# Cross-attention's softmax division moved from the attention result to the output weight's products, and its key sums taken with a column of ones

## The chip, the cores and the metric

One core of a Trainium2 chip runs the whole program. The metric is device time in microseconds of that core, as the median of several executions. The unprofiled executions of the kernel before lie between 1841.42 and 1842.9 us.

## The reference, cut to what matters

A decoder of two layers works on `x` of 4 batches, 256 tokens, 256 features. The first five sublayers and the last one are: rotary self-attention, cross-attention to `ctx` without weights, a ternary feed-forward, a gated recurrence, then the cross-attention that the change is in, then a mixture of 8 experts with the best 2 taken. The cross-attention of the second layer, with 16 query heads of 128 features that share 4 key and value heads, is:

```python
q = (draft_hidden @ Wq.T).reshape(bsz, draft_len, H, HD)         # H = 16, HD = 128, 256 queries
q = _rms_norm(q, q_norm_w).transpose(0, 2, 1, 3)
kv_in = jnp.concatenate([context_hidden, draft_hidden], axis=1)  # 1601 + 256 = 1857 keys
k = (kv_in @ Wk.T).reshape(bsz, total_len, KVH, HD)              # KVH = 4
v = (kv_in @ Wv.T).reshape(bsz, total_len, KVH, HD).transpose(0, 2, 1, 3)
k = _rms_norm(k, k_norm_w).transpose(0, 2, 1, 3)
q = _rope(q, draft_position_ids)
k = _rope(k, full_position_ids)
k = jnp.repeat(k, N_REP, axis=1)                                 # N_REP = 4
v = jnp.repeat(v, N_REP, axis=1)
scores = jnp.einsum('bhqd,bhkd->bhqk', q, k) * SCALE
probs = jax.nn.softmax(scores, axis=-1)
attn = jnp.einsum('bhqk,bhkd->bhqd', probs, v)
attn = attn.transpose(0, 2, 1, 3).reshape(bsz, draft_len, H * HD)
return attn @ Wo.T                                               # added to x by the caller
```

The mixture of experts follows it per batch and needs the finished `x` of that batch.

## The kernel before, in words

Everything is float32. Up to about 500 us four generators, one for each batch, run the first four sublayers interleaved. After that comes the cross-attention, which takes the largest part of the time.

The cross-attention loops over 16 "heads" `(b, g)`: batch `b`, key-value head `g`. Each has two `Pair` objects, `h = 0` and `h = 2`, and a pair holds two query heads with 256 queries each, so 512 query columns. There are 32 pairs. The 1857 keys are in 15 chunks of up to 128, taken two at a time in `NPAIR = 8` steps.

- `Pair.score(c)` multiplies a chunk of keys by the 512 queries into a PSUM bank `bsc` (L1181). ScalarE copies it to `s` with the key's norm as the scale (L1182), and VectorE keeps a running maximum `acc` over chunks (L1186). Keys stand on partitions, queries on the free axis.
- `Pair.maximum()` transposes `acc` (`tm`, L1193), takes the maximum of each query (`mq`, L1195) and spreads it again over partitions into the bank `bc` (L1199).
- `Pair.exponential(c)` subtracts `bc` (VectorE, L1203), takes the exponential (ScalarE, L1206) and adds it to `sum` (GpSimd, L1212), a 128 by 512 tile that has one partial sum for each partition of keys.
- `Pair.weigh(c)` multiplies values by `s` into the bank `po` (L1221): 128 value features on partitions, 512 queries on the free axis.
- `Pair.finish()` is what the change is in. It copies `po` to `aT` (ScalarE, L1228). It transposes the four 128-column blocks of `sum` into a bank `ts` (L1232), so that queries stand on partitions, reduces over the free axis (VectorE, L1234) and takes the reciprocal `rs` (L1235). It spreads `rs` over partitions by four transposes into a bank `rb` (L1239) and multiplies `aT` by it (L1240). In pair `h = 2` of a head, all four query heads' `aT` are multiplied by the output weight `wo` into one bank `bpw`, accumulating over the four heads (L1247), and one VectorE add puts the bank into `x` (L1252).

A float32 product is two TensorE instructions in the trace; a transpose is one.

Between these, a head's successor is prepared: `prep_q` (queries, `pq` L1078, rotary, then `ACT L1047` scales by a norm that GpSimd works out at L1043, then `tpq` L1090 and the copy L1091) and `prep_kv` (keys and values, `pk` L1115, rotary, `tpk` L1124, and the copy of the keys `kTb` by ScalarE, L1126). The experts of the batch before run in 23 steps (`mph` L914, `mpe` L925, and an addition to `x` of a product scaled per token, L927).

The order of all this is written out by hand. Work runs in steps `s`; a step has two places, `2s` after the scores and `2s + 1` after the weighing. `put(place, gen, last, bank)` books the next part of a generator at a place; with `bank=True` it takes the first place from there on that no other booking with `bank=True` holds. [...] 32 places make one head, and a head lasts about 82 us in the trace.

[...] one for `bc`, one for `po`, and six that `p1(...)` hands out in turn. So a bank from `p1` can be written only when what was handed out six requests earlier has been read. `ts`, `rb`, `bpw`, `bsc`, `tm`, `pq`, `pk`, `tpk`, `mph` and `mpe` all come from `p1`.

`load_wo` loads the head's output weight; its booking is 15 places ahead of the place of `rb` in the pair `h = 0`.

Of the kernel before, what the change touches and what calls it, by code (L numbers as in the profile page):

```python
# [16 lines left out]
ALU = mybir.AluOpType  # L17
AX = mybir.AxisListType
PSUM = bass.MemoryType.PSUM

P = 128
# [88 lines left out]
def decoder_kernel(ctx: ExitStack, tc: tile.TileContext, at, t, out):  # L110
    nc = tc.nc
    V, A, G, T = nc.vector, nc.scalar, nc.gpsimd, nc.tensor
# [18 lines left out]
    def p1(name):  # L131

        ring[0] += 1
        if psb and ring[0] % 3 == 0:
            return psb[0].tile([P, 512], F32, tag="one", name=name, bufs=2)
        return psa.tile([P, 512], F32, tag="one", name=name, bufs=4)
# [17 lines left out]
    def fa(b, name, dt=F32):  # L154

        return fr.tile([P, 512], dt, tag=f"a{b}", name=name, bufs=NA)
# [9 lines left out]
    def sm(shape, tag, name, bufs=2, dt=F32):  # L166
        return small.tile(shape, dt, tag=tag, name=name, bufs=bufs)
# [3 lines left out]
    xs = [const.tile([P, 2, D], F32, tag=f"x{b}", name=f"x{b}") for b in range(B)]  # L171
# [14 lines left out]
    def cc(name):  # L186
        o, n = at[name]
        return cst[:, o : o + n]

    ident = cc("ident")  # L190
# [768 lines left out]
    def angles(b):  # L959

        d = bt.setdefault(b, {})
        pi = wk.tile([P, NCH], I32, tag="pi", name=f"pi{b}")
        nc.sync.dma_start(out=pi, in_=t["pos"][b])
        if b == 0:
            V.tensor_scalar(knw, knw, math.sqrt(HD1), None, ALU.mult)
        pf = wk.tile([P, NCH], F32, tag="pf", name=f"pf{b}")
        V.tensor_copy(pf, pi)
        sh = [P, NCH, 64]
        ang, sn = (
            fr.tile([P, 960], F32, tag=n, name=f"{n}{b}")[:, 0 : NCH * 64].rearrange(  # L970
                "p (a b) -> p a b", a=NCH
            )
            for n in ("ang", "sn")
        )
        V.tensor_mul(ang, pf[:, :, None].to_broadcast(sh), cc("invf")[:, None, :].to_broadcast(sh))
        yield
        V.tensor_scalar(sn, ang, 1.0 / (2 * math.pi), ROUND, ALU.mult, ALU.add)
        yield
        V.tensor_scalar(sn, sn, ROUND, None, ALU.subtract)
        yield  # L980
        for c in TWO_PI:
            V.scalar_tensor_tensor(ang, sn, -c, ang, ALU.mult, ALU.add)
            yield
        V.tensor_scalar(ang, ang, PI_LO, -PI_LO, ALU.min, ALU.max)
        yield
        A.activation(sn, ang, AF.Sin)
        A.activation(ang, ang, AF.Abs)
        A.activation(ang, ang, AF.Sin, bias=hpi, scale=-1.0)
        d["angles"] = (ang, sn)
        yield  # L990

    def tables(b, only="kq"):

        d = bt[b]
        ang, sn = d["angles"]
        for nm, n, w in (("k", NCH, knw), ("q", 2, qnw)):
            if nm not in only:
                continue
            tb = [P, n, 64]
            ctab = wk.tile([P, n, HD1], F32, tag=f"c{nm}", name=f"ctab{nm}{b}")  # L1000
            stab = wk.tile([P, n, HD1], F32, tag=f"s{nm}", name=f"stab{nm}{b}")
            wlo, whi = w[:, None, 0:64].to_broadcast(tb), w[:, None, 64:128].to_broadcast(tb)
            d[nm] = (ctab, stab)
            V.tensor_mul(ctab[:, :, 0:64], ang[:, 0:n, :], wlo)
            V.tensor_mul(ctab[:, :, 64:128], ang[:, 0:n, :], whi)
            yield

            V.scalar_tensor_tensor(stab[:, :, 64:128], sn[:, 0:n, :], -1.0, whi, ALU.mult, ALU.mult)
            V.tensor_mul(stab[:, :, 0:64], sn[:, 0:n, :], wlo)
            yield  # L1010
# [149 lines left out]
    class Pair:  # L1160
# [62 lines left out]
        def finish(self):  # L1223
            b, g, nm = self.b, self.g, self.nm
            e, su = gt[b, g], self.sum
            aT = fa(1, f"aT{nm}")
            e[self.h] = aT
            A.copy(aT, self.po)  # L1228
            yield
            ts = p1(f"ts{nm}")  # L1230
            for i in range(4):
                T.transpose(ts[:, i * P : (i + 1) * P], su[:, i * P : (i + 1) * P], ident)  # L1232
            rs = sm([P, 4], "rs", f"rs{nm}")
            V.tensor_reduce(rs, ts.rearrange("p (i k) -> p i k", i=4), AX.X, ALU.add)  # L1234
            V.reciprocal(rs, rs)  # L1235
            yield
            rb = p1(f"rb{nm}")
            for i in range(4):
                T.transpose(rb[:, i * P : (i + 1) * P], rs[:, i : i + 1].to_broadcast([P, P]), ident)  # L1239
            V.tensor_mul(aT, aT, rb)  # L1240
            yield
            if self.h == 2:
                pw = p1(f"bpw{b}{g}")
                for j in range(2):
                    for h in range(4):
                        o = (h % 2) * 256 + j * P
                        T.matmul(  # L1247
                            pw[:, j * 256 : j * 256 + 256], lhsT=e[h - h % 2][:, o : o + P], rhs=e["wo"][:, h, :],
                            start=h == 0, stop=h == 3,
                        )  # L1250
                xf = xs[b].rearrange("p j d -> p (j d)")
                V.tensor_add(xf, xf, pw)  # L1252


    heads = [(b, g) for b in range(B) for g in range(NKV)]
# [11 lines left out]
    def put(place, gen, last=False, bank=False):  # L1267
        while bank and place in taken:
            place += 1
        if bank:  # L1270
            taken.add(place)
        places.setdefault(place, []).append((gen, last))
        return place

    def loader(b, g):
        load_wo(b, g)
        yield

    def tokens(b):
        normed_tokens(b)  # L1280
        yield
        bt[b]["xh"] = bt[b]["centred"]()
        yield
        token_features(b)
        yield

    for n, pair in enumerate(pairs):
        e = NPAIR * n + NPAIR - 1
        gen = pair.maximum()
        put(2 * e + 2, gen, bank=True)  # L1290
        put(2 * e + 5, gen, True)
        e += DW
        gen = pair.finish()
        put(2 * e + 1, gen)
        put(2 * e + 4, gen, bank=True)
        put(2 * e + 7, gen, pair.h == 0, bank=True)
        if pair.h:
            put(2 * e + 10, gen, True, bank=True)
    for k, (b, g) in enumerate(heads):
        base = 32 * (k - 1)  # L1300
        if k:
            if g == 0:
                gen = angles(b)
                for i in range(9):
                    put(base - 81 + 6 * i, gen, i == 8)
                gen = tokens(b)
                for i, o in enumerate((-8, -6, -3)):
                    put(base + o, gen, i == 2, i == 2)
                for o, n in ((-5, "q"), (-3, "q"), (7, "k"), (11, "k")):
                    gen = tables(b, n) if o in (-5, 7) else gen  # L1310
                    put(base + o, gen, o in (-3, 11))
            for f, when in ((prep_q, QA), (prep_kv, KA)):
                for i, o in enumerate(when):
                    gen = f(b, g, i)
# [4 lines left out]
        gen = loader(b, g)  # L1319
        put(base + 60, gen, True)  # L1320
    for b in range(B - 1):
        gen = experts(b)
# [145 lines left out]
```

## Time and profile before

| what | value |
|---|---|
| median of the executions | 1842.06 us (1841.42 to 1842.9) |
| profiled execution, its own time | 1839.59 us |
| span in its profile | 1837.7 us |
| what lies around the span | 1.89 us |
| granted TensorE clock, mean | 0.971 |
| TensorE matmul busy | 1727.6 us (94%) |
| VectorE busy | 1288.4 us (70%) |
| ScalarE busy | 1007.2 us (55%) |
| GpSimd busy | 871.8 us (47%) |

A profile is of one execution. Its span is from the first to the last instruction; the time of that execution adds what lies around it. The profiled execution is 2.47 us below the median of the unprofiled ones, so a difference worked out from the profile is subtracted from or added to the median as it stands. The row of an instruction gives its duration from start to end; TensorE overlaps one instruction with the next, so its pace is read from the starts of successive instructions and not from durations. PE is TensorE's matmul, PEld its weight load, DVE is VectorE, ACT ScalarE, POOL GpSimd and SP SyncE, which issues the DMAs.

### The profile page before, as it was taken

How to read it: one execution, taken by the hardware profiler on the slowest of the kernel's cores; microseconds unless marked ns; L12 is line 12 of the kernel's file. 1: busy time of each engine (PE TensorE's matmuls, PEld its weight loads, DVE VectorE, ACT ScalarE, POOL GpSimd, SP SyncE). 2: the span in 40 equal slices, each digit the busy share in tenths (PEclk: the TensorE clock that was granted, in tenths of full speed). 3: DMA queues.
4: the chain of work that ended last, by engine and by line, in shares of the span. 5: the costliest groups of instructions: out<-in, count | busy, mean ns of one | idle time of the engine just before them, and what ended most of it. 6: DMA issues, size and time to landing. Idle time of an engine off the chain costs nothing.

```text
span 1837.7 us, 20229 instructions
## 1 busy us (share of the span) xinstructions
PE 1727.6 (94%) x6576; PEld 1051.1 (57%) x6576; DVE 1288.4 (70%) x2396; ACT 1007.2 (55%) x1896; POOL 871.8 (47%) x716
## 2 busy tenths in 40 slices
PE   4779899989999999999999999999999999999997
PEld 3456786655555554645555555656565655656555
DVE  5785647787777677777767786776768676766754
ACT  1556536464656555675656566565746465555631
POOL 2100232111277566566656465555647574555560
PEclk8789899999999999999999999999999999999998
DMA  4010231100210110102010111201111211111110
GB/s 139 1 39 17 73 119 61 32 24 25 67 55 15 52 34 33 38 30 65 17 62 27 63 35 49 61 29 55 34 62 33 68 38 52 32 35 44 32 38 23
DMA packets 66216, 83.00 MB, mean 45 GB/s; under 512 B 6460, under 2 KB 49600, under 8 KB 66112
## 3 DMA queue, kind: packets, MB, share of 16 engines
q1 hardware_dynamic: 64960, 80.31, 14.1%
q10 hardware_dynamic: 1152, 1.41, 0.2%
q8 instruction: 53, 0.87, 0.2%
q14 instruction: 51, 0.42, 0.1%
HBM read 80.65 MB, written 1.05 MB: 44 GB/s over the span
## 4 chain that ended last, share of the span: by engine, by line
PE 72%; DVE 10%; ACT 8%; POOL 6%; issue 4%; POOLq 0%; DVEq 0%; ACTq 0%
PE bsc L1181 18%; PE bpo L1221 17%; PE pk L1115 11%; POOL sum L1212 3%; PE bpw L1247 3%; PE mph L914 2%; PE xpo L607 2%; ACT s L1206 2%; PE xsc L562 2%; ACT s L1182 2%; PE pq L1078 2%; PE mpe L925 1%; ACT sm L463 1%; PE pp L689 1%; PE tpk L1124 1%
## 5 line engine op out<-in xcount | busy, mean ns | idle before, releaser
L1212 POOL TENSOR_TENSOR sum<-sum,s 128x512 f32<-128x512 f32 (+1 forms) x416 | 541.0, 1301 | 81.9 <-ACT s L1206 55.5
L1181 PE MATMUL bsc<-qTb,kTb 128*128 128x512 f32 (+1 forms) x960 | 457.9, 597 | 3.3 <-ACT kTb L1126 3.3
L1221 PE MATMUL bpo<-s,vb 128*128 128x512 f32 (+1 forms) x960 | 456.0, 593 | 0.0
L1182 ACT ACTIVATE s<-bsc,kn 128x512 f32<-128x512 f32 (+1 forms) x480 | 317.8, 685 | 186.1 <-PE bsc L1181 164.4
L1186 DVE SCALAR_TENSOR_TENSOR acc<-bsc,kn,acc 128x512 f32<-128x512 f32 x448 | 333.6, 745 | 110.0 <-ACT s L1182 100.4
L1203 DVE TENSOR_TENSOR s<-s,bc 128x1024 f32<-128x1024 f32 (+1 forms) x256 | 288.4, 1141 | 14.2 <-PE bc L1199 14.0
L1206 ACT ACTIVATE s<-s 128x1024 f32<-128x1024 f32 (+1 forms) x256 | 256.1, 1009 | 60.7 <-DVE s L1203 59.9
L1181 PEld LDWEIGHTS bsc<-qTb,kTb 128*128 128x128 f32 (+1 forms) x960 | 172.1, 187 | 187.8 <-issue 145.8
L1221 PEld LDWEIGHTS bpo<-s,vb 128*128 128x128 f32 (+1 forms) x960 | 173.4, 191 | 141.3 <-issue 136.6
L1040 POOL TENSOR_TENSOR ropek<-ropek,ropuk 128x512 f32<-128x512 f32 (+1 forms) x64 | 76.9, 1201 | 255.9 <-DVE ropuk L1035 255.9
L1115 PE MATMUL pk<-wkv,cTk 128*128 128x256 f32 x832 | 190.1, 379 | 0.0
L1115 PEld LDWEIGHTS pk<-wkv,cTk 128*128 128x128 f32 x832 | 156.7, 190 | 28.4 <-issue 6.2
L1209 POOL TENSOR_TENSOR sum<-s 128x512 f32<-128x512 f32 x32 | 41.8, 1306 | 186.7 <-ACT s L1206 186.7
L1034 DVE TENSOR_TENSOR ropek<-pk,ctabk 128x256 f32<-128x256 f32 (+1 forms) x128 | 51.8, 404 | 70.6 <-ACT squares L1033 69.9
L1033 ACT ACTIVATE squares<-pk 128x256 f32<-128x256 f32 (+1 forms) x128 | 48.1, 377 | 96.3 <-PE pk L1115 74.7
L1047 ACT ACTIVATE ropeq<-ropeq,rnq 128x128 f32<-128x128 f32 x128 | 41.9, 390 | 107.4 <-POOL rnq L1043 107.4
L1184 DVE TENSOR_SCALAR acc<-bsc,kn 128x512 f32<-128x512 f32 x32 | 24.0, 749 | 83.5 <-ACT s L1182 83.5
L1118 ACT COPY vb<-pk 128x256 f32<-128x256 f32 (+1 forms) x128 | 46.3, 362 | 58.7 <-DVE ropuk L1035 56.0
L463 ACT ACTIVATE sm<-sc,mx 128x128 f32<-128x128 f32 (+1 forms) x128 | 52.2, 435 | 26.5 <-DVE mx L456 19.6
L1043 POOL TENSOR_TENSOR kn<-ssk,nhalf 128x4 f32<-128x4 f32 (+1 forms) x64 | 65.5, 1024 | 0.0
L914 PE MATMUL mph<-yTm,wi 128*128 128x256 f32 x256 | 63.2, 392 | 0.0
L1040 POOL TENSOR_TENSOR ropeq<-ropeq,ropuq 128x512 f32<-128x512 f32 x32 | 41.1, 1284 | 40.5 <-DVE ropuq L1035 40.5
(491 smaller groups left out, 2482.8 us busy)
## 6 DMA issues: line engine op xcount, KB each, us to landing
cTk<-in_ctxT SPq DMA_DIRECT2D x32, 512.0 KB, 3.6
wq<-in_wq SPq DMA_DIRECT2D x16, 512.0 KB, 4.9
wo<-in_wo SPq DMA_DIRECT2D x16, 512.0 KB, 4.0
wi<-in_wi SPq DMA_DIRECT2D x32, 256.0 KB, 2.9
xcT<-in_ctxT SPq DMA_DIRECT2D x12, 512.0 KB, 3.7
xct<-in_ctx SPq DMA_DIRECT2D x12, 512.0 KB, 3.7
cTk<-in_ctxT SPq DMA_DIRECT2D x16, 384.0 KB, 3.2
wkv<-in_wkv SPq DMA_DIRECT2D x16, 256.0 KB, 3.8
```

The source lines that it names most:

```text
L463: A.activation(ex[:, h, k], scs[u][:, h, k], AF.Exp, bias=mx[:, j, i : i + 1], accum_out=sums[:, j, i : i + 1])
L914: T.matmul(ph[:, i * 256 : i * 256 + 256], lhsT=wi[:, i, c, f * ME : (f + 1) * ME], rhs=yT[:, c, :], start=c == 0, stop=c == 1,)
L1040: G.tensor_tensor(r4, r4, u4[:, :, ::-1, :], ALU.add)
L1043: G.tensor_tensor(rn, ss[:, 0:n], nhalf[:, 0:n], ALU.pow)
L1115: T.matmul(pk[:, q, :], lhsT=src, rhs=e["wkv"][:, c, :], start=c == 0, stop=c == 1)
L1181: T.matmul(pc[0:n, :], lhsT=e["kT"][:, k * P : k * P + n], rhs=q, start=True, stop=True)
L1182: A.activation(s[0:n, i, :], pc[0:n, :], AF.Copy, scale=e["kn"][0:n, k : k + 1])
L1186: V.scalar_tensor_tensor(self.acc[0:n, :], pc[0:n, :], e["kn"][0:n, k : k + 1], self.acc[0:n, :], ALU.mult, ALU.max)
L1203: V.tensor_tensor(s[0:n, 0:w, :], s[0:n, 0:w, :], self.bc[0:n, None, :].to_broadcast([n, w, 512]), ALU.subtract)
L1206: A.activation(s[0:n, 0:w, :], s[0:n, 0:w, :], AF.Exp)
L1212: G.tensor_tensor(self.sum[0:n, :], self.sum[0:n, :], s[0:n, i, :], ALU.add)
L1221: T.matmul(self.po, lhsT=e["v"][0:n, k, :], rhs=self.s[c][0:n, i, :], start=k == 0, stop=k == NCH - 1)
```

## The change

The four transposes of `sum` and the reduction become four products of a 128-column block of `sum`, as the stationary operand, with one column of ones: each gives one column of `ts`, the sum over keys with queries on partitions. The reciprocal reads these four columns from PSUM. The spreading of `rs` and the multiplication of `aT` go. The products with `wo` are done for one query head at a time, in each pair, into a bank of its own, and are not accumulated over heads in PSUM. VectorE scales each half of the bank by the queries' reciprocal and adds it to `x` in one instruction. Both pairs of a head now book four parts; before, `h = 0` had three.

```diff
             aT = fa(1, f"aT{nm}")
-            e[self.h] = aT
             A.copy(aT, self.po)
             yield
             ts = p1(f"ts{nm}")
             for i in range(4):
-                T.transpose(ts[:, i * P : (i + 1) * P], su[:, i * P : (i + 1) * P], ident)
+                T.matmul(ts[:, i : i + 1], lhsT=su[:, i * P : (i + 1) * P], rhs=cc("ones")[:, 0:1], start=True, stop=True)
             rs = sm([P, 4], "rs", f"rs{nm}")
-            V.tensor_reduce(rs, ts.rearrange("p (i k) -> p i k", i=4), AX.X, ALU.add)
-            V.reciprocal(rs, rs)
-            yield
-            rb = p1(f"rb{nm}")
-            for i in range(4):
-                T.transpose(rb[:, i * P : (i + 1) * P], rs[:, i : i + 1].to_broadcast([P, P]), ident)
-            V.tensor_mul(aT, aT, rb)
-            yield
-            if self.h == 2:
-                pw = p1(f"bpw{b}{g}")
+            V.reciprocal(rs, ts[:, 0:4])
+            yield
+            for h in range(2):
+                pw = p1(f"bpw{nm}{h}")
                 for j in range(2):
-                    for h in range(4):
-                        o = (h % 2) * 256 + j * P
-                        T.matmul(
-                            pw[:, j * 256 : j * 256 + 256], lhsT=e[h - h % 2][:, o : o + P], rhs=e["wo"][:, h, :],
-                            start=h == 0, stop=h == 3,
-                        )
-                xf = xs[b].rearrange("p j d -> p (j d)")
-                V.tensor_add(xf, xf, pw)
+                    o = h * 256 + j * P
+                    T.matmul(
+                        pw[:, j * 256 : j * 256 + 256], lhsT=aT[:, o : o + P], rhs=e["wo"][:, self.h + h, :], start=True, stop=True
+                    )
+                for j in range(2):
+                    V.scalar_tensor_tensor(
+                        xs[b][:, j, :], pw[:, j * 256 : j * 256 + 256], rs[:, 2 * h + j : 2 * h + j + 1], xs[b][:, j, :], ALU.mult, ALU.add
+                    )
+                yield
...
         put(2 * e + 4, gen, bank=True)
-        put(2 * e + 7, gen, pair.h == 0, bank=True)
-        if pair.h:
-            put(2 * e + 10, gen, True, bank=True)
+        put(2 * e + 7, gen, bank=True)
+        put(2 * e + 10, gen, True, bank=True)
```

## The prediction

> **What bounds the kernel now.** I read busy times and slices first, then the waits, then the timeline around the lines that change.
>
> ```profile
> PE 1727.6 (94%) x6576; PEld 1051.1 (57%) x6576; DVE 1288.4 (70%) x2396; ACT 1007.2 (55%) x1896; POOL 871.8 (47%) x716
> PE   4779899989999999999999999999999999999997
> ```
>
> From slice 12 on, which is the cross-attention, PE is the wall; no other engine is near it. So two things count: PE's issue time, and the moments when PE stands. PE's pace is read from starts: four 512-column products take 1.72 us (0.43 each), sixteen `bpw` products of 256 columns 3.46 (0.216 each), four transposes 0.44 (0.109 each). I summed these spacings over PE's starts from 500 to 1780 us: 1253 of 1280 us are issue time, and 26.7 us are stalls, ahead of `bsc` 7.3, `bc` 6.2, `rb` 6.0, `tpk` 4.5, `tm` 1.5 and the rest 1.2. Most `rb` stalls have one form. The timeline at the first:
>
> ```profile
> 557.58 0.17 DVE L1235 RECIPROCAL rs<-rs 128x4 f32<-128x4 f32 x1
> 557.80 0.65 PE L1239 MATMUL rb<-cst,rs 128*128 128x128 f32 x4 [0.94 <-DVE rs L1235]
> 558.13 0.43 ACT L1126 COPY kTb<-tpk 128x321 f32<-128x321 f32 x1
> 558.61 1.98 PE L1181 MATMUL bsc<-qTb,kTb 128*128 128x512 f32 x4 [0.15 <-ACT kTb L1126]
> ```
>
> PE waits 1.11 us for the reciprocal; VectorE is late because it had waited 4.29 us for ScalarE. Right after, PE waits 0.32 more for the key copy that the same busy ScalarE makes. This second limit matters: removing the first wait alone would lead PE straight into it. The waits in total:
>
> ```profile
> DVE x L1252 <- PE bpw L1247: 29.2, 16, 3.0
> PEld bsc L1181 <- ACT kTb L1126: 14.9, 27, 2.0
> PEld rb L1239 <- DVE rs L1235: 12.0, 11, 1.8
> ```
>
> Columns: us in total, times, longest. PEld's waits overlap PE's running products, so 12.0 is more than PE loses.
>
> [...] I price by the trace throughout.
>
> **The change part by part.**
>
> 1. *Key sums on PE.* Four products with one column are eight instructions, each with a 128-column weight load. Nothing with one column runs in this stage; the nearest row is the router's eight-column product:
>
> ```profile
> 892.84 0.95 PE L869 MATMUL pl<-wgt,yTm 128*128 128x8 f32 x8
> 893.65 1.53 PE L1181 MATMUL bsc<-qTb,kTb 128*128 128x512 f32 x3
> ```
>
> Eight take 893.65 - 892.84 = 0.81 us. They replace four transposes of 0.44: +0.37 a pair. `rb` goes: -0.44 a pair. Times 32 pairs: 11.8 - 14.0 = **-2.0 us** of issue time. Bounds: [...] if the sums overlapped down to the old transposes, -14; if each stepped like a 256-column product, 0.216, then +27, for which I see no reason.
>
> 2. *Output products.* Per head 16 instructions of 256 columns before and after, 3.46 us: 0. But their place moves: half of them go from pair `h = 2` to pair `h = 0`, two places each (`A` where `rb` was, `B` three places later), 0.86 us a place.
>
> 3. *VectorE.* Rows:
>
> ```profile
> L927 DVE SCALAR_TENSOR_TENSOR x<-mpe,gts,x 128x256 f32<-128x256 f32 x64 | 27.8, 476 | 11.1 <-PE mpe L925 10.4
> L1240 DVE TENSOR_TENSOR aT<-aT,rb 128x512 f32<-128x512 f32 x32 | 21.8, 680 | 4.3 <-PE rb L1239 4.1
> L1234 DVE TENSOR_REDUCE rs<-ts 128x4 f32<-128x512 f32 x32 | 21.8, 680 | 6.7 <-PE ts L1232 6.7
> L1252 DVE TENSOR_TENSOR x<-x,bpw 128x512 f32<-128x512 f32 x16 | 11.0, 688 | 29.2 <-PE bpw L1247 29.2
> ```
>
> Per head: off 2 x 0.680 + 2 x 0.680 + 0.688 = 3.41; on 8 x 0.476 = 3.81; the reciprocals stay (0.17, [...]). So +0.4 a head, +6.4 us in all, on an engine at 70%: 0, hidden by PE. Without that cover it is +6.4.
>
> 4. *Stalls.* I take the late engine's time as fixed and count how much more PE has to do before it meets it. In pair `h = 0` that is +0.37 after the sums, +0.80 after `A` (0.37 + 0.86 - 0.44), +1.67 after `B`; pair `h = 2` has 1.73 less. Head by head:
> - 558, 637, 879, 1218, 1555: `rb` 1.1 and `bsc` 0.3 each, and 801: `bsc` 1.9. PE no longer needs `rs`, but it meets `kTb`. Gain 0.80 each, 4.8.
> - 962, 1134, 1301, 1471, 1637: `tpk`, 0.6 to 1.0, waiting for GpSimd, behind the sums only. Gain 0.37 each, 1.9. The `rb` stall after the one at 1134, 0.31, goes.
> - 735, 1068, 1405: `bc`, 2.65, 2.51, 0.87, five places after `B`. PE has 1.67 more to do, VectorE 0.54 more (4 x 0.476 against 2 x 0.680). Gain 1.1, 1.1, 0.87, so 3.1.
>
> Together **-10.1 us**. Pair `h = 2` has no such stalls: its `bpw` burst is followed by 3.46 us of `pk`, in which ScalarE idles 4.49 us at 1015, so taking 1.73 us of PE work from it opens nothing as far as I see. The lower bound of the gain is 1 (the late engines are pushed back by what PE does more), the upper 16 (all of `rb`, its `bsc` and most of `bc`).
>
> 5. *New wait.* VectorE now waits for `A` and `B`. Behind it stand the next `s` subtraction and `acc`, behind those ScalarE's exponential, and `bpo` one step later. Before, VectorE stood about 1.8 us at each `bpw` (29.2 / 16), and no PE stall followed one. `A` ends 0.43 later than `rb` did. I charge **+2**, bounds 0 and +13 (32 x 0.4).
>
> 6. *Banks.* A pair asks `p1` for 3 banks instead of 2.5. `ts` is free one reduction (0.68) earlier, a `bpw` bank is held for half as long. 0, inside the charge above.
>
> 7. *Moved bookings.* `B` of `h = 0` takes places that experts' steps held: of batches 0 to 2, steps 3 to 7, 10, 11, 15, 16, 20 and 21 come one place later, some two (2.6 us each). None issues on GpSimd. Steps 7, 11 and 15 issue expert weight loads on SP; step 7's pass one `wo` load, which may wait in the queue, but SP runs ahead: it issued a `wo` at 1013.39, some 30 places before its booking. First use of `wo` is now 15 places (38 us) after its booking, against a landing of 4.0. The experts of a batch end far ahead of the next. 0, bounds -1 to +3.
>
> 8. *The end.* The last sums wait for GpSimd:
>
> ```profile
> 1791.42 1.12 PE L1232 MATMUL ts<-cst,sum 128*128 128x128 f32 x4 [3.16 <-POOL sum L1212]
> 1794.81 0.69 DVE L1240 TENSOR_TENSOR aT<-aT,rb 128x512 f32<-128x512 f32 x1 [1.34 <-PE rb L1239]
> 1795.56 2.86 PE L1247 MATMUL bpw<-wo,aT 128*128 128x256 f32 x12 [0.85 <-DVE aT L1240]
> 1798.45 0.69 DVE L1252 TENSOR_TENSOR x<-x,bpw 128x512 f32<-128x512 f32 x1 [2.95 <-PE bpw L1247]
> ```
>
> `x` is done at 1799.14. After: sums eight times, about 0.2 each since PE's first products there step 0.427 (half pace after the idle), 1793.1; then four products for each of `A` and `B`, at 0.427 to 0.216, 1.7 to 3.4 together, and two scaled additions after the last, 1.0 with the latency: 1795.8 to 1797.5. Gain 1.6 to 3.3; I take **-2**.
>
> Sum: -2.0 - 10.1 + 2 - 2 = -12.1. Item 4 assumes fixed late engines at fourteen places; I keep three quarters of it, -7.6, so **-9.6 us**. The profiled execution of 1839.59 becomes 1830.0; it lies 2.47 below the median, which becomes 1842.06 - 9.6 = 1832.5.
>
> **Rivals.** A measurement of this kernel can tell about 0.2%, 3.7 us, from no change.
> - *Forecast* (0.68): stalls shrink as in 4; 1825 to 1838.
> - *The stalls only move* (0.18): PE leaves `rb` and stands at `kTb`, whose 14.9 us the change does not touch. Then items 1 and 8 are left, against the charge of 5: -4 + 2 = -2, 1840. For it speaks that ScalarE copies `kTb` at 558.13 whatever PE does; against it, that the moved products fill that very gap.
> - *VectorE holds the exponentials* (0.14): `A` stands at the end of a step, just ahead of the next subtraction. If VectorE is less than a step ahead of `bpo`, each of 32 pairs loses up to the 0.86 of `A`: +27; at half of them +14, less 4 from items 1 and 8: +10, 1852. It decides from a `bpo` stall of 0.4 us a pair on. Against it: `bpo` stalls sum to 0.8 us now, even after the 1.8 us holds at `bpw`.
> - That the change doesn't do what it says is not open: the diff removes `rb` and its two users whole.
>
> The range 1824 to 1843 takes in the first two and leaves out most of the third. Faster 0.69, same 0.17, slower 0.14.
>
> **What would show it.** Right: no `rb` stall; `ts` eight products in 0.81 us; PE's stalls in the stage near 19 us; `bsc` waiting for `kTb` shorter; VectorE's busy time up some 6 us; waits of `x` for `bpw` about as long in total as 29.2, split over 64. Wrong: `ts` products 0.2 apart at full clock (item 1), PE waiting ahead of `bpo` for ScalarE's exponentials (item 5), `bc` waiting longer for `mq` (item 3), or expert steps waiting for weights (item 7).

## The result, and the profile after

| | before | changed |
|---|---|---|
| median of the executions | 1841.2 us (1838.07 to 1842.9, 6 runs) | 1831.2 us (1825.66 to 1832.09, 6 runs) |
| ratio to before | 1 | 0.9944, 95% interval 0.9931 to 0.9958 |
| profiled execution, its own time | 1839.59 us | 1831.5 us |
| span | 1837.7 us | 1829.5 us |

The change is 10.0 us faster by the medians (forecast: 9.6), 7.7 to 12.7 by the interval. The page's first two views look almost the same as before: VectorE is busy for 12.1 us more, and PE is as full as it was.

```profile
PE 1727.7 (94%) x6576; PEld 1054.0 (58%) x6576; DVE 1300.5 (71%) x2444; ACT 1008.2 (55%) x1896; POOL 872.4 (48%) x716
PE   3779899989999999999999999999999999999997
```

That page cannot say where 8.2 us of span went. The pace of PE can. The table below takes PE's starts from the first `bc` to the last `ts`, and splits each start-to-start interval into the steady spacing of its kind (issue) and what is over it (stall). "End" runs from the start of the last `ts` to the first transpose of the last experts. All in us, one profiled execution each; the experiments' rows are used further down.

| kernel | stage | issue | stalls | `rb` | `bsc` | `bc`, `tm` | `tpk` | last `ts` | end |
|---|---|---|---|---|---|---|---|---|---|
| before | 1291.6 | 1260.9 | 30.1 | 6.0 | 7.3 | 7.7 | 4.5 | 3.3 | 10.6 |
| changed | 1285.7 | 1263.4 | 21.9 | - | 6.3 | 9.3 | 2.1 | 1.8 | 7.2 |
| e1 sums only | 1301.4 | 1275.0 | 26.0 | 0.0 | 8.5 | 10.9 | 2.2 | 3.0 | 12.0 |
| e2 division only | 1276.4 | 1249.3 | 26.5 | - | 8.9 | 9.7 | 4.2 | 2.1 | 7.1 |
| e3 late products | 1299.2 | 1261.7 | 37.0 | - | 16.3 | 13.8 | 2.1 | 3.5 | 10.9 |
| e4 last head only | 1291.5 | 1262.5 | 28.4 | 6.0 | 7.2 | 7.7 | 4.5 | 1.8 | 6.6 |
| e5 both at once | 1277.2 | 1249.1 | 27.6 | - | 6.2 | 11.2 | 4.2 | 2.1 | 7.7 |
| e6 old bookings | 1283.2 | 1263.2 | 19.6 | - | 6.3 | 7.2 | 2.1 | 1.8 | 8.2 |
| e7 scaled twice | 1287.4 | 1263.4 | 23.5 | - | 10.2 | 7.2 | 2.1 | 1.8 | 10.2 |
| e8 queries earlier | 1276.4 | 1248.0 | 27.9 | - | 10.4 | 10.0 | 4.2 | 2.0 | 6.1 |
| e9 fewer sums | 1273.4 | 1263.4 | 9.6 | - | 4.8 | 0.4 | 2.1 | 1.8 | 8.9 |
| e10 division, old bookings | 1275.0 | 1249.1 | 25.4 | - | 9.1 | 8.4 | 4.2 | 2.1 | 6.1 |

Issue includes 1.7 us in the changed kernel that only moved across the border: the products of the last head's first pair now stand ahead of the last `ts`. (In e8 it is the other way round: 1.3 us of work that was booked earlier falls ahead of the first `bc`.) After some waits of the stage PE runs at half pace for 3.41 us, with a granted clock of 0.5 and 512-column products 0.85 us apart instead of 0.43. That counts as a stall in the column where it falls: 1.7 us in the kernel before, which has one such stretch in the stage (from 736.0), and 3.3 us in the changed one, which has two (from 737.9 and from 1069.0).

The first part of the run, up to the first `bc`, has the same code in all of these kernels and ended between 495.5 and 502.0 us; in the changed kernel's profile it ended 1.5 us later than in that of before. So the span's -8.2 is 1.5 (first part) - 5.8 (stage) - 3.4 (end) - 0.4 (last experts), up to rounding.

The place of the first `rb` stall, in the timeline of the changed kernel (start, duration, engine; in brackets the idle time before it and what ended it):

```profile
558.63 1.03 PE L1241 MATMUL bpw<-wo,aT 128*128 128x256 f32 x4
559.62 0.43 ACT L1126 COPY kTb<-tpk 128x321 f32<-128x321 f32 x1
560.10 1.98 PE L1181 MATMUL bsc<-qTb,kTb 128*128 128x512 f32 x4 [0.44 <-ACT kTb L1126]
```

Before, PE stood 1.11 + 0.32 us here. Now it runs four output products, by their pace up to 559.50, and stands 0.60 for the key copy. The wait moved to the rival's place, `kTb`, and more than half of it was filled.

The waits (us in total, times, longest):

```profile
PEld bsc L1181 <- ACT kTb L1126: 15.5, 28, 1.0
DVE x L1245 <- PE bpw L1241: 12.3, 18, 1.3
PE bc L1199 <- DVE mq L1195: 7.3, 3, 3.7
```

VectorE waits less for the products than before (29.2): a burst is 4 instructions long and not 16. The `bc` wait got longer (5.5 before).

The groups of the changed lines:

```profile
L1245 DVE SCALAR_TENSOR_TENSOR x<-bpw,rs,x 128x256 f32<-128x256 f32 x128 | 55.5, 474 | 12.4 <-PE bpw L1241 12.3
L1234 DVE RECIPROCAL rs<-ts 128x4 f32<-128x4 f32 x32 | 5.5, 172 | 5.8 <-PE ts L1232 5.8
L1232 PE MATMUL ts<-cst,sum 128*128 128x1 f32 x256 | 30.4, 240 | 1.6 <-POOL sum L1212 1.6
```

The scaled additions cost what the experts' row said (0.474 against 0.476), and the reciprocal from PSUM 0.172 (0.166 before, from `rs`).

The one-column products, in the timeline:

```profile
552.26 0.95 PE L1232 MATMUL ts<-cst,sum 128*128 128x1 f32 x8
553.07 1.96 PE L1221 MATMUL bpo<-s,vb 128*128 128x512 f32 x4
554.87 0.59 PE L1181 MATMUL bsc<-qTb,kTb 128*128 128x512 f32 x1
```

The eight take 0.81 us from start to start, as forecast. But the four products behind them take 554.87 - 553.07 = 1.80 us and not 1.72: the first of them holds PE 0.513 us instead of 0.429.

The end:

```profile
1787.10 1.05 PE L1232 MATMUL ts<-cst,sum 128*128 128x1 f32 x8 [1.60 <-POOL sum L1212]
1788.01 2.60 PE L1241 MATMUL bpw<-wo,aT 128*128 128x256 f32 x8
1789.16 0.88 DVE L1245 SCALAR_TENSOR_TENSOR x<-bpw,rs,x 128x256 f32<-128x256 f32 x2 [0.79 <-PE bpw L1241]
1790.65 0.88 DVE L1245 SCALAR_TENSOR_TENSOR x<-bpw,rs,x 128x256 f32<-128x256 f32 x2 [0.61 <-PE bpw L1241]
```

From the last `ts` to the finished `x` it is 4.43 us; before it was 7.72.

### The profile page after: what moved, and what is told of

The parts are those of the page before. It is cut to its first block, busy times and chain, and to the rows that moved or that the text cites. A ratio compares the mean times of both kernels' runs of the same rounds, so it can differ in the third digit from the quotient of the medians.

```text
span 1829.5 us, 20298 instructions
## 1 busy us (share of the span) xinstructions
PE 1727.7 (94%) x6576; PEld 1054.0 (58%) x6576; DVE 1300.5 (71%) x2444; ACT 1008.2 (55%) x1896; POOL 872.4 (48%) x716
## 3 DMA queue, kind: packets, MB, share of 16 engines
HBM read 80.65 MB, written 1.05 MB: 45 GB/s over the span
## 4 chain that ended last, share of the span: by engine, by line
PE 70%; DVE 10%; ACT 8%; POOL 7%; issue 4%; DMA 0%; POOLq 0%; ACTq 0%; DVEq 0%
PE bsc L1181 17%; PE bpo L1221 17%; PE pk L1115 11%; POOL sum L1212 4%; PE mph L914 2%; PE bpw L1241 2%; ACT s L1206 2%; PE xsc L562 2%; ACT s L1182 2%; PE xpo L607 2%; PE pq L1078 1%; PE mpe L925 1%; ACT sm L463 1%; POOL ropeq L1040 1%; ACT ropeq L1047 1%
## 5 line engine op out<-in xcount | busy, mean ns | idle before, releaser
L1241 PEld LDWEIGHTS bpw<-wo,aT 128*128 128x128 f32 x256 | 48.7, 191 | 34.2 <-issue 27.0
L1241 PE MATMUL bpw<-wo,aT 128*128 128x256 f32 x256 | 66.3, 382 | 0.0
```

The lines of the kernel that those rows point to most:

```text
L1241: T.matmul(pw[:, j * 256 : j * 256 + 256], lhsT=aT[:, o : o + P], rhs=e["wo"][:, self.h + h, :], start=True, stop=True)
```

## The experiments

The theory after the result: PE's issue time and PE's stalls add up; the output products stand where PE had waited for late engines; the end is a serial chain that got shorter. Each comparison below is with runs of the kernel before on the same chip, whose medians lay between 1840.8 and 1842.1 us.

### e1 and e2: the two halves of the change apart

e1, on the kernel before:

```diff
-                T.transpose(ts[:, i * P : (i + 1) * P], su[:, i * P : (i + 1) * P], ident)
+                T.matmul(ts[:, i : i + 1], lhsT=su[:, i * P : (i + 1) * P], rhs=cc("ones")[:, 0:1], start=True, stop=True)
             rs = sm([P, 4], "rs", f"rs{nm}")
-            V.tensor_reduce(rs, ts.rearrange("p (i k) -> p i k", i=4), AX.X, ALU.add)
-            V.reciprocal(rs, rs)
+            V.reciprocal(rs, ts[:, 0:4])
```

> The kernel before with only the key sums done as products with one column of ones; the division stays where it was, by transposes and a multiplication of aT. Theory (PE's issue time sets the stage): eight one-column products step 28 ns once and 112 ns after that, and the product behind them starts 84 ns late, so 0.90 us a pair against 0.44 for four transposes: +14.7 us of issue time in 32 pairs. VectorE loses a reduction of 0.68, so the reciprocal comes about 0.2 us earlier and some of the six rb stalls shrink: -2. Slower than before by 10 to 15 us. Rival one (the sums hide in PE's stalls): within 4 us of before. Rival two (the shorter VectorE work is what made the changed kernel faster): faster than before by 3 us or more.

Measured: 1850.26 us, ratio 1.0054 (1.0042 to 1.0067), so 9.9 us slower. Issue rose by 14.1. All of `rb`'s 6.0 us of stalls went, because the reciprocal comes earlier (at the first place at 556.60 instead of 557.58) and PE gets to `rb` later. `bsc`, `bc` and `tm` gave 4.4 of it back, and the end cost 1.4 more. The estimate lies a hair under the 10 to 15 expected, the interval reaches into it; both rivals are out.

e2 is the changed kernel with this same edit reversed.

> The changed kernel with the key sums taken as before, by four transposes and a reduction; the division stays on the output products. Theory (PE's issue time sets the stage, the sums by products cost 0.46 us a pair more than transposes): the changed kernel's 10 us gain, 14.7 us of issue time on top, 2 to 3 us given back at the key copies because PE reaches them earlier: 18 to 25 us faster than before, likeliest 21. VectorE's busy time is 16 us above the changed kernel's and hidden. Rival (the stage is held by other engines' lateness, so shorter PE work only lengthens stalls): about 10 us faster than before, like the changed kernel, with PE's stalls up by 10 us or more.

Measured: 1819.77 us, ratio 0.9889 (0.9876 to 0.9903), so 20.4 us faster than before by the ratio, 21.1 by the medians. Issue is 14.1 below the changed kernel's, stalls are 4.6 above. The theory's number holds. The key sums by one-column products are thus a loss in both settings, about 10 us, and the division on the output products, with the places that it takes, a gain of about 20.

### e3: the products back in the second pair

On the changed kernel (the first pair's two places stay booked and are empty):

```diff
-            for h in range(2):
+            e[self.h] = aT, rs
+            for q in (0, 2):
+                for h in range(2 if self.h else 0):
...
                 yield
```

> The changed kernel with the output products of both pairs of a head done in the second pair, two heads' products at each of its two places; the first pair's two places are booked and empty. Sums, scaling and count of instructions are those of the changed kernel. Theory (moving half of the products into the first pair fills PE's stalls there): the wait for the key copy behind the emptied place comes back by up to 0.86 us in six heads, 3 to 5 us, and the end has two heads' products more, 0.9 to 1.7 us: 4 to 7 us slower than the changed kernel, so 3 to 6 us faster than before. Rival (only the removed wait for the reciprocal counts, the place of the products does not): the end's 0.9 to 1.7 us alone, 8 to 9 us faster than before, and no longer stalls ahead of bsc.

Measured: 1846.92 us, ratio 1.0034 (1.0022 to 1.0046), 6.3 us slower than before. The sign is the theory's, the size is beyond it: some 16 us are lost against the changed kernel, not 4 to 7. In the timeline of PE of e3:

```profile
557.98 1.98 PE L1181 MATMUL bsc<-qTb,kTb 128*128 128x512 f32 x4 [1.30 <-ACT kTb L1126]
```

and in its waits:

```profile
PEld bsc L1181 <- ACT kTb L1126: 30.1, 34, 2.1
```

With nothing between `bpo` and `bsc` PE stands there, at this first place for 1.46 us, about as long as the 1.11 + 0.32 of the kernel before. It does so in eleven heads by 0.43 us or more, and not in six: stalls ahead of `bsc` rise from 6.3 to 16.3 us (1.4 of the rise is half pace), ahead of `bc` and `tm` from 9.3 to 13.8, and the end is 3.7 longer. So taking PE's wait for `rs` away is worth nothing by itself; the work that stands in its place is. e3 also brings the products of four heads close together in the second pair; how much of the loss ahead of `bc` comes from that was not tried.

### e4: the end alone

On the kernel before, the changed `finish` and its bookings for the last two pairs:

```diff
-        gen = pair.finish()
+        new = n >= len(pairs) - 2
+        gen = pair.finish_new() if new else pair.finish()
...
-        put(2 * e + 7, gen, pair.h == 0, bank=True)
-        if pair.h:
+        put(2 * e + 7, gen, pair.h == 0 and not new, bank=True)
+        if pair.h or new:
```

> The kernel before, with the changed form in the last head alone (two of 32 pairs). Theory (the end of the attention, which waits for the last GpSimd sum, is a serial chain; the changed form takes a reduction, four transposes, a multiplication and half of the products off it): from the start of the last sums to the finished x 4.4 us instead of 7.7, so 3 to 4 us faster than before, and no difference up to there. Rival (the end hides in the experts' loads and clock): within 1 us of before.

Measured: 1835.57 us, ratio 0.9974 (0.9963 to 0.9984), 4.8 us faster with an interval of 2.9 to 6.8. The stage is the same to 0.1 us (1291.5), the end falls from 10.6 to 6.6. The rival is out. Shown: the end alone is worth about 4 us; in the changed kernel it is 3.4 of the 10.

### e5: both of the first pair's products ahead of the key copy

On e2:

```diff
-                yield
+                if self.h or h:
+                    yield
...
-        put(2 * e + 7, gen, bank=True)
-        put(2 * e + 10, gen, True, bank=True)
+        put(2 * e + 7, gen, pair.h == 0, bank=True)
+        if pair.h:
+            put(2 * e + 10, gen, True, bank=True)
```

> The kernel with the division alone moved (sums by transposes), and in the first pair both heads' output products at the first of the two places, right ahead of the wait for the key copy; the second pair keeps its two places. Counts and issue time are those of the division alone. Theory (products in front of that wait fill it): stalls ahead of bsc fall from 8.9 us by 4 to 6 us, so 25 to 27 us faster than before where the division alone was 21. Rival (VectorE, which then has four scaled additions in a row, holds the exponentials): stalls ahead of bpo of 5 us or more, and no faster than the division alone.

Measured: 1820.65 us, ratio 0.9883 (0.9867 to 0.9898), no different from e2. Neither theory holds whole. The `bsc` waits did shrink as expected where they were looked for (1.05 to 0.17 us at the first), 8.9 to 6.2 in all, and `bpo` stalls came to no more than 0.4. But 2.1 us came up ahead of `tpq`, which was not there before, and 1.5 more ahead of `bc` and `tm`. What is gained at the first late engine is lost at the next.

### e6: the experts' steps at their old places

On the changed kernel:

```diff
-        put(2 * e + 10, gen, True, bank=True)
+        put(2 * e + 10, gen, True, bank=pair.h == 2)
```

> The changed kernel with the last part of the first pair put at its place without booking it, so that the experts' steps stand at the places that they had before. Theory (the shift of those steps by one or two places is worth nothing): 8 to 12 us faster than before, like the changed kernel. Rival (the shift gives part of the gain, or costs part of it): more than 3 us off the changed kernel.

Measured: 1829.57 us, ratio 0.9934 (0.9921 to 0.9946), 12.2 us faster than before, a hair beyond the 8 to 12 expected. Its interval overlaps the changed kernel's, so the times do not show that the shift costs anything; by the ratios it would be some 2 us. The traces do show one place where a shifted step stands in the way, at the second change of batch. In the timelines of ScalarE and PE of the changed kernel, and in that of PE of e6:

```profile
1064.51 0.36 ACT L919 ACTIVATE it<-mph 128x256 f32<-128x256 f32 x1
1068.04 0.65 PE L1199 MATMUL bc<-cst,mq 128*128 128x128 f32 x4 [3.68 <-DVE mq L1195]
```

```profile
1065.03 0.65 PE L1199 MATMUL bc<-cst,mq 128*128 128x128 f32 x4 [1.81 <-DVE mq L1195]
```

In the changed kernel the experts' step (L919) comes on ScalarE behind the scaling by the query norm, and VectorE waits for it on the way to the maximum: from the end of the norm on GpSimd to `bc` it takes 4.74 us. In e6 L919 is done at 1054.61, well ahead, and it takes 3.32, as in the kernel before. The stalls ahead of `bc` and `tm` are 7.2 instead of 9.3, and the same edit on e2 (e10) takes them from 9.7 to 8.4.

### e7: VectorE's new work doubled

On the changed kernel, ahead of each scaled addition:

```diff
+                    V.scalar_tensor_tensor(
+                        scr, pw[:, j * 256 : j * 256 + 256], rs[:, 2 * h + j : 2 * h + j + 1], xs[b][:, j, :], ALU.mult, ALU.add
+                    )
```

> The changed kernel with every scaled addition done twice, the first time into a bf16 tile that nobody reads: 128 more VectorE instructions of about 0.47 us, 60 us of busy time more. Theory (VectorE's own work hides behind PE): the doubled work sits in the first pairs too, where VectorE is late, so a small part shows: 0 to 8 us slower than the changed kernel. Rival (VectorE's 0.4 us a head more counts in full): 60 us slower than the changed kernel; or half of that where VectorE is the late one at half of the places.

Measured: 1833.64 us, ratio 0.9953 (0.9938 to 0.9967), 8.7 us faster than before and, by the ratios, about 2 slower than the changed kernel, whose interval it overlaps. Its page:

```profile
PE 1728.1 (94%) x6576; PEld 1056.8 (58%) x6576; DVE 1352.8 (74%) x2572; ACT 1006.0 (55%) x1896; POOL 874.6 (48%) x716
```

52.3 us more of VectorE cost some 2, if anything, within the theory's 0 to 8; both rivals are out. The cover that the prediction claimed is there. What shows is an end that is 3.0 us longer, stalls ahead of `bc` and `tm` that are 2.1 shorter, and 3.9 us more ahead of `bsc`, nearly all of it at one place:

```profile
1064.06 2.08 PE L1183 MATMUL bsc<-qTb,kTb 128*128 128x512 f32 x2 [3.43 <-DVE x L1250]
```

L1250 is a scaled addition in this kernel. It writes nothing that `bsc` reads, so PE waits for the PSUM bank that the addition still has to read; the addition stood behind an experts' step (L920) that had kept VectorE waiting 5.38 us for ScalarE.

### e8 and e9: the wait ahead of `bc`

The prediction had this wait shrink, and it grew. The changed kernel's first one, in the timelines of GpSimd, ScalarE, VectorE and PE:

```profile
720.73 10.91 POOL L1212 TENSOR_TENSOR sum<-sum,s 128x512 f32<-128x512 f32 x7 [1.88 <-ACT s L1206]
731.61 1.26 POOL L1040 TENSOR_TENSOR ropeq<-ropeq,ropuq 128x512 f32<-128x512 f32 x1
732.83 1.02 POOL L1043 TENSOR_TENSOR rnq<-ssq,nhalf 128x4 f32<-128x4 f32 x1
```

```profile
733.88 0.98 ACT L1047 ACTIVATE ropeq<-ropeq,rnq 128x128 f32<-128x128 f32 x3 [8.01 <-POOL rnq L1043]
```

```profile
735.47 0.75 DVE L1184 TENSOR_SCALAR acc<-bsc,kn 128x512 f32<-128x512 f32 x1 [4.95 <-ACT s L1182]
736.13 0.68 DVE L1195 TENSOR_REDUCE mq<-tm 128x4 f32<-128x512 f32 x1
```

```profile
736.87 0.65 PE L1199 MATMUL bc<-cst,mq 128*128 128x128 f32 x4 [2.83 <-DVE mq L1195]
```

Read from the bottom: PE waits for VectorE's maximum, that stands behind an `acc` which waits for ScalarE, ScalarE stands 8.01 us for the query norm (`rnq`), and GpSimd has seven sums in a row ahead of the query's addition and the norm. In the kernel before:

```profile
721.04 8.19 POOL L1212 TENSOR_TENSOR sum<-sum,s 128x512 f32<-128x512 f32 x5 [1.89 <-ACT s L1206]
730.41 1.26 POOL L1212 TENSOR_TENSOR sum<-sum,s 128x512 f32<-128x512 f32 x1
```

There five sums stood ahead of the addition, which lies between these two rows, and a sixth ahead of the norm. So the norm now has one sum of 1.3 us more ahead of it, and at the other two changes of batch as well. e8 books the second half of the query preparation three places earlier, on e2:

```diff
-    QA, KA, HB, HC = (2, 6), (11, 13, 15, 17), 5, 8
+    QA, KA, HB, HC = (2, 5), (11, 13, 15, 17), 5, 8
```

> The kernel with the division alone moved, and the second half of the query preparation booked three places earlier. The waits ahead of bc, 8.0 us in three batch changes, come from ScalarE standing for the norm of the second half of the queries, which GpSimd works out behind the sums. Theory (it is late because it starts late): stalls ahead of bc fall from 8.0 to below 3, 24 to 27 us faster than before. Rival (it is late because GpSimd has seven sums ahead of it in any case, or other waits open where the preparation now stands): stalls ahead of bc stay, within 3 us of the division alone or slower.

Measured: 1822.81 us, ratio 0.9896 (0.988 to 0.9911), as fast as e2; stalls ahead of `bc` 8.3. The rival holds: seven sums stand ahead of the norm again, and booking it earlier doesn't help. e9 takes the sums away instead, on the changed kernel:

```diff
-                for i in range(w):
+                for i in range(1 if (self.b, self.g, self.h) in ((0, 2, 2), (1, 2, 2), (2, 2, 2)) else w):
                     G.tensor_tensor(self.sum[0:n, :], self.sum[0:n, :], s[0:n, i, :], ALU.add)
```

> The changed kernel with GpSimd's sum of the second chunk left out from the second step on, in three of 32 pairs (the second pair of head 2 in batches 0, 1 and 2, whose sums run ahead of the three long bc waits): 6 additions of 1.3 us each less there, 7.8 us; the three pairs' key sums lack those chunks. Theory (the chain at the change of batch is: PE waits for the maximum, VectorE for ScalarE, ScalarE for the query norm of GpSimd, and that stands behind the sums): the waits ahead of bc fall from 8.0 us to below 2, 4 to 8 us faster than the changed kernel, so 14 to 18 us faster than before. Rival (ScalarE's wait ends with something else, or the time is taken up by the next wait): stalls ahead of bc above 5 us, within 2 us of the changed kernel.

Measured: 1819.26 us, ratio 0.9883 (0.9866 to 0.9899), 21.5 us faster than before, beyond the 14 to 18 expected. Its wait for the query norm:

```profile
ACT ropeq L1047 <- POOL rnq L1043: 104.1, 32, 4.9
```

The longest was 8.4 in the changed kernel. Stalls ahead of `bc` fell to 0.1 and all stalls from 21.9 to 9.6. More came than the waits ahead of `bc` and `tm`, 8.9 us, because the half pace behind them went too, 3.3 us; the end was 1.7 longer. The length of PE's wait does not decide alone whether half pace follows. In the kernel before, it followed a wait for `mq` of 2.49 us and not one of 2.35; in the changed kernel it followed waits of 2.83 and 3.68 us and not one of 0.78; in e2 it followed none of the three, of which the longest was 3.2. What sets it off these runs do not show. Shown: three bursts of sums on an engine at 48%, and the half pace behind them, hold PE for some 10 us.

### e10: the two best edits together

> The division alone moved (sums by transposes), with the last part of the first pair not booked, so that the experts' steps stand at their old places: the two edits that were best by themselves. Theory (they add): 21 us of the division alone and the 1 to 2 us by which the old bookings were ahead of the changed kernel, 21 to 24 us faster than before. Rival (the 1 to 2 us were noise, or the waits are met elsewhere): 19 to 21 us.

The edits are those of e2 and e6. Measured: 1816.55 us, ratio 0.9871 (0.9855 to 0.9887), 23.7 us faster than before by the ratio, the lowest median of all. Its interval overlaps that of e2, so that the bookings add something is not shown. Its profile is of an execution whose first part, with unchanged code, ended 4.4 us earlier than that of before (495.5 against 499.9). Stage and end together, which leave this out, are 2.4 us below those of e2 (1281.1 against 1283.5).

## Why the prediction was right, point by point

1. *Key sums on PE.* Forecast -2.0 us, in truth about +0.8. The step that failed is "Eight take 893.65 - 892.84 = 0.81 us. They replace four transposes of 0.44: +0.37 a pair". The 0.81 was met; but the successor of the product behind the eight starts 0.084 late, so a pair pays 0.896 against 0.436, +0.46. e1 and e2 both have 14.1 us of issue time for it. It could have been seen in the very line that the prediction showed: the three 512-column products behind the eight had 1.53 us, and three others have 1.45. A small slip of the sum beside it: 11.8 - 14.0 is -2.2 as printed (the unrounded steps give -2.0).
2. *Output products.* Issue time unchanged, as said. That their place matters was the centre of item 4, and e3 shows it.
3. *VectorE.* 12.1 us more busy time instead of 6.4. Added up by durations, overlaps counted twice, it is 16.0 us more: the changed lines have 6.3 of them, as forecast, and the rest is in instructions that did not change but lasted longer, most of them small, such as the router's (the eight of L879 took 3.7 us together and not 1.4). Why they did was not settled. The work is hidden, as e7 shows.
4. *Stalls.* Forecast -10.1, of which three quarters were kept, -7.6. Without the last `ts`, measured 26.8 to 20.1: -6.7. By group: `rb` with `bsc` -7.0 (forecast -5.1), `tpk` -2.4 (forecast -1.9), `bc` with `tm` +1.6 (forecast -3.1), and 0.9 new ahead of the experts' products, at half pace after a `bc` wait. The term that failed is "Gain 1.1, 1.1, 0.87, so 3.1": the three `bc` stalls were to shrink from 2.65, 2.51 and 0.87 us to about 1.55, 1.4 and 0, and they measured 3.00, 3.84 and 0.94. It took the late engines' times as fixed. In the changed kernel one sum more, 1.3 us, stands ahead of the query norm at each of the three places, and at the second an experts' step adds 1.4 us (e6). A longer wait of `bc` for `mq` was named among the signs of being wrong, but for VectorE's work; the chain that e8 and e9 follow leads to GpSimd.

   The edit touches no line that GpSimd runs, and none of the moved steps has work for it, so the order in which an engine gets its instructions is not that of the kernel's text alone. The norm has the additional sum in e1, e2 and e6 too, and not in e4: either half of the change, made in every pair, is enough for it, and the bookings are not needed. What sets that order was not tried.
5. *New wait.* Charged +2, cost nothing: `bpo`'s stalls stayed at 0.8. Two signs of the last paragraph did not come: `x` waits for `bpw` 12.3 us in total and not about 29.2, and the weight loads' waits for `kTb` did not get shorter in total (15.5 against 14.9), though the longest did.
6. *Banks.* Nothing in the waits of the changed kernel points to them. With VectorE's work doubled (e7), one wait of 3.43 us for a bank appears; their number was not tried by itself.
7. *Bookings.* Forecast 0. The times of e6 leave room for a cost of some 2 us without showing it. The traces show 1.4 us at the second `bc`, a way that the prediction did not list.
8. *The end.* Forecast -2, measured -3.4, and 1.5 less waiting for the last sum. The term that was mis-sized is "sums eight times, about 0.2 each": they took 0.91 us (1787.10 to 1788.01) and not 1.7. What follows, 3.5 us to the finished `x`, lies inside the 2.7 to 4.4 that were given.

So the total hit, but not each term, and that it hit so closely is partly luck: the misses cancel. From the first `bc` on the profiles show -9.7 (5.8, 3.4 and 0.4 before rounding) against the -9.6 forecast: item 1 is 2.8 worse and item 4 is 0.9 worse, item 5 is 2 better and the end with the last experts 1.9 better; the 1.7 us of products that moved ahead of the last `ts` were nearly paid by its shorter wait, 1.5. Within item 4, `bc` is 4.7 worse and the half pace 0.9, `rb` with `bsc` and `tpk` are 2.4 better, and the 2.5 withheld cover most of the rest. What was right is the mechanism that decides: the products that moved into the first pair fill PE's waits (e3), and VectorE's work is covered (e7). Of the rivals, "the stalls only move" is half true, at `kTb`, and e3 shows what it would have looked like without the moved products; "VectorE holds the exponentials" is out.

## What to carry to other kernels

When PE waits for a late engine, ask what PE meets right after that wait is gone; here it was another wait of the same length (1.46 us in e3 for the 1.11 + 0.32 before), and only work moved into that place paid. A one-column product in place of a transpose saves a reduction elsewhere, but here it costs PE 0.112 us per instruction, two per product in float32, where a transpose is one instruction of 0.109: in this kernel, bound by PE, the transpose and a reduction on an engine with time to spare are cheaper. An engine at 48% can still hold everything for 3 us, as GpSimd does here, where seven sums, 10.91 us in a row, stand ahead of a norm of 1.02 us that others wait for.

## What was not expected of the hardware

In the trace of the changed kernel, after a group of eight instructions of one column the next 512-column product occupies PE for 0.513 us instead of 0.429, in all 30 groups that one follows; the two that are followed by a 256-column product show 0.300 instead of 0.216. The router's eight-column groups show the same 0.513 at the three places where a 512-column product follows. Within the group the second instruction starts 0.028 us after the first and the others step 0.112; in the last group, for which PE had stood idle 1.60 us, the first step is 0.133. Counted together a group costs PE eight steps of 0.112, 0.896 us.
